# Moving a recurrence's result transposes one step later in an interleaved two-layer Flamingo kernel

## The chip, the cores and the metric

One Trainium2 chip, one of its cores. The metric is device time in microseconds of one execution, median over runs; lower is better. The engines are PE (TensorE, matrix products and transposes), DVE (VectorE), ACT (ScalarE), POOL (GpSimd) and SP (SyncE, which here issues the DMA transfers). [...]

## What is computed

The input x is 4 batch elements of 512 tokens with 512 channels, with a context of the same shape. Two layers follow each other, each a mixing step and a feed-forward step, with gates:

```python
x = x + tanh(g_xattn[0]) * wkv(w, u, layernorm(x), ctx)          # recurrence over tokens
x = x + tanh(g_ffn[0])   * ffn(layernorm(x), w1, w2, w3)          # 512 -> 2048 -> 512
x = x + tanh(g_xattn[1]) * attention(layernorm(x), ctx, wq, bq, wkv, bkv, wp, bp)  # 16 heads
x = x + tanh(g_ffn[1])   * ternary(x, gamma, W)                   # 512 -> 512

# wkv, per channel and token t, with k = layernorm(x), v = ctx
no  = max(o, u + k);  A  = exp(o - no);      E  = exp(u + k - no)
y   = (A * p + E * v) / (A * q + E)
no2 = max(w + o, k);  A2 = exp(w + o - no2); E2 = exp(k - no2)
p, q, o = A2 * p + E2 * v, A2 * q + E2, no2

# ffn: activations rounded to int8 in groups of 64, weights sign(w) * mean|w|
h = silu(bitlinear(x, w1)) * bitlinear(x, w2);  out = bitlinear(h, w3)
```

The attention rounds its query and output inputs per token and those weights per output channel to int8; the ternary step does the same for activations and takes weights to -1, 0, 1.

## The kernel before

P is 128. NB = 4 elements, each 4 token tiles of 128 (NT) by 4 channel blocks of 128 (NC); the hidden 2048 are 4 blocks of 512 (NF).

**The layers.** `wkv_layer` (L551) holds one element's recurrence with channels on partitions and tokens along the row, as 4 chunks of 128 channels (`chunk`, L576). One chunk: a scan on DVE for the running maximum (L588), a subtraction on POOL (L597), ReLUs and exponentials on ACT (L601, L603) into a tile `wk_e` with four 512-long rows, two more scans on DVE (L618, L623), a reciprocal in two halves on DVE (L629), and the product y (L634), which overwrites one row of `wk_e`. PE then transposes y into one PSUM bank `wy_ps` (L636 to L638), and DVE multiplies by the gate and adds into the state `xb` (L640). `wk_e` has a single buffer for elements 1 to 3. For elements 1 to 3 the four chunks are chained by `in_steps(chains, 8)`: chunk c + 1 begins 8 steps after chunk c, and where two chunks have work in one step, the later chunk goes first.

`ffn_layer` (L690) runs 16 units per element, one per (token tile t, hidden block f), in four steps each: `up(t, f, 0)` into a bank `ff_hp` by 8 products, with `gate` behind it (tanh on ACT, L731; DVE, L732); `down` of the unit before the last, 8 products into `ff_acc`, and at f = 3 the addition to `xb` (L759); `up(t, f, 1)` with `gated` (DVE L736 and `quantised`: DVE L231 and L662 to L666, ACT L670, POOL L671); and `gate_parts` of the unit before, which transposes its `ff_z` (`tp_ps`) and splits it in two parts (`hr`: ACT L682, DVE L683). The first element is run with `made`, an object that fetches the weights, takes their signs or rounds them, and turns them, while the units run.

`attention_layer` (L815) is prepared per token tile (`prepared`, L840) and then runs 16 units of (head pair, half), each 8 parts: a score product into a bank `s_ps`, its negative maximum on DVE (`at_nm`, L929), the exponential on ACT (`at_P`, L931), 4 transposes into a bank `pt_ps`, a copy out of it (`at_PT`, L951 on ACT), products with the values (`o_ps`), and a last product and scaling (`ot_ps`, `at_o`, L989). `ternary_layer` (L1123) closes an element.

**The order of the work.** All layers are generators, and each `yield` ends a step. `line` (L1165) gives a generator's steps places on a common scale in which an element's FFN takes 16 of 17 slots; `run` (L1149) always takes the step with the smallest place. Thus FFN of element b + 1, attention of b and recurrence of b + 2 run together. A chunk's eight steps stand 0.05 slot behind FFN steps' places, an attention step 0.05 slot ahead:

```python
(b - 1.0 + 5.05 / SLOTS, b - 1.0 + 13.05 / SLOTS, 32),   # recurrence of b: 4 chunks of 8 steps
(b, b + 16 / SLOTS, 64),                                  # FFN of b: 16 units of 4 steps
start = b + 1 + 4.95 / SLOTS                              # attention of b: 72 steps from here
```

PE's order between steps is written out by hand: `matmul` (L167) and `transpose` (L170) pass each instruction through `in_turn`, and `next_turn` makes what follows stand behind what came before. The order on DVE, ACT, POOL and SP is chosen when the program is built, within the data's dependences and the buffers.

**The banks.** PSUM tiles come from rings by tag: `m` (all transposes by `bank`, and `o_ps`), `hp` (`ff_hp` and `s_ps`) and `acc`:

```python
psum["now"] = boot_ps, {"m": 2, "hp": 2, "acc": 4}   # first element
psum["now"] = ps, {"m": 3, "hp": 3, "acc": 2}        # from then on
```

A tile takes the bank of the one that came so many tiles of its tag before it, and so waits for that one's last reader. For elements 2 and 3 the order on PE around a chunk's end is: `tp_ps`, `wy_ps`, two `s_ps`, `ff_hp` of the next unit's first up, `o_ps`, two `pt_ps`, `ff_acc`.

**Two smaller pieces.** `output_scales` (L424) spreads the weights' scales `sp` (one value per partition and column j) over the rows: a DVE copy `w_full` (L429) of column j broadcast to 128 by 128, then its transpose into `pb_ps` (L430), then a gate product (L431). It runs near the end of the first element (unit 14.7), just after `ternary`, which takes wf to -1, 0, 1 on DVE (L235 to L237) for the transposes `wt_ps`. `prepared` does the same for a token tile's scale: POOL writes `at_full` (L848) into a row ring of three buffers (`at_row`, shared with `at_xn`, `at_q` and `at_half`), PE transposes it into `sx_ps`, and ACT copies it out (L853).

Of the kernel before, what the change touches and what calls it, by code (L numbers as in the profile page):

```python
# [10 lines left out]
F32 = mybir.dt.float32  # L11
# [5 lines left out]
ALU = mybir.AluOpType  # L17
# [4 lines left out]
P = 128  # L22
# [8 lines left out]
def kernel(  # L31
# [36 lines left out]
    nc = tc.nc  # L68
# [68 lines left out]
    def bank(name, dtype=F32):  # L137

        return psum_tile(name, "m", dtype)
# [30 lines left out]
    def transpose(*args):  # L170
        return in_turn(nc.tensor.transpose(*args))  # L171
# [119 lines left out]
    class Weights:  # L291
# [132 lines left out]
        def output_scales(self):  # L424

            pb = bank("pb_ps")
            for j in range(NC):
                full = self.pool.tile([P, P], F32, name="w_full", tag="w_full", bufs=2)
                nc.vector.tensor_copy(full, self.sp[:, j : j + 1].to_broadcast([P, P]))  # L429
                transpose(pb[:, j * P : (j + 1) * P], full, ident)  # L430
            nc.vector.tensor_scalar(swp_b, pb, gates[:, 1:2], None, ALU.mult)  # L431
            nc.sync.dma_start(out=bp_b, in_=bcast(bp))
            nc.vector.tensor_scalar(bp_b, bp_b, gates[:, 1:2], None, ALU.mult)
# [117 lines left out]
    def wkv_layer(b, xb):  # L551

        kT = wk.tile([P, NC, T], F32, name=f"wk_k{b}", tag="wk_k")
        if b:
            r = layernorm(xb, pinned=True)
            yield  # L560
        else:
            r = layernorm(xb)
        for t in range(NT):
            if b or t == 0:
                xn = wk.tile([P, D], F32, name="wk_xn", tag="wk_v")
            else:
                xn = ff.tile([P, D], F32, name="wk_xn", tag="ff_a", bufs=3)
            centred(xn, xb, r, t)
            yield
            pt = bank("wk_ps")  # L570
            for c in range(NC):
                transpose(pt[:, c * P : (c + 1) * P], xn[:, c * P : (c + 1) * P], ident)
            nc.scalar.copy(kT[:, :, t * P : (t + 1) * P], blocks(pt))  # L573

        def chunk(c):
            def row(name):  # L576
                if b == 0 and c % 3:
                    return ff.tile([P, T + 1], F32, name=name, tag=(None, "ff_a", "xp")[c % 3], bufs=3)
                return wk.tile([P, T + 1], F32, name=name, tag=name)

            if b > 1:
                v = wk.tile([P, T], F32, name="wk_v", tag="wk_v")
                nc.sync.dma_start(out=v, in_=cD[b][:, c, :])
            k = kT[:, c, :]
            w_c, u_c, w_n, u_n = (a[:, c : c + 1] for a in (wc, uc, wcn, ucn))
            o = row("wk_o")
            nc.gpsimd.memset(o[:, 0:1], NEG_INF)
            nc.vector.tensor_tensor_scan(  # L588
                o[:, 1:], w_c.to_broadcast([P, T]), k, NEG_INF, ALU.add, ALU.max
            )  # L590

            if b == 0 and c < 3:
                e = ring.tile([P, 4, T], F32, name="wk_e", tag="w")
            else:
                e = wk.tile([P, 4, T], F32, name="wk_e", tag="wk_e")
            z = row("wk_p")[:, 0:T]
            nc.gpsimd.tensor_tensor(z, k, o[:, 0:T], ALU.subtract)  # L597
            if b:
                yield True
            for i, (sign, at) in enumerate(((1.0, u_c), (-1.0, w_c), (-1.0, u_n), (1.0, w_n))):  # L600
                nc.scalar.activation(e[:, i, :], z, AF.Relu, bias=at, scale=sign)  # L601
                if b and i % 2:
                    nc.scalar.activation(  # L603
                        e[:, i - 1 : i + 1, :], e[:, i - 1 : i + 1, :], AF.Exp, scale=-1.0
                    )
                    yield True
            if b == 0:
                exps[c] = nc.scalar.activation(e, e, AF.Exp, scale=-1.0)
                yield True

            A, E2, E, A2 = (e[:, i, :] for i in range(4))
            if b < 2:
                v = context.cT[b][:, c, :]
            q = row("wk_q")
            p = row("wk_p")
            nc.gpsimd.memset(q[:, 0:1], 0.0)
            nc.gpsimd.memset(p[:, 0:1], 0.0)  # L617
            nc.vector.tensor_tensor_scan(q[:, 1:], A2, E2, 0.0, ALU.mult, ALU.add)  # L618
            nc.gpsimd.tensor_tensor(E2, E2, v, ALU.mult)
            den = q[:, 0:T]  # L620
            nc.vector.tensor_tensor(den, A, den, ALU.mult)
            yield True
            nc.vector.tensor_tensor_scan(p[:, 1:], A2, E2, 0.0, ALU.mult, ALU.add)  # L623
            nc.gpsimd.tensor_tensor(den, den, E, ALU.add)
            nc.gpsimd.tensor_tensor(E, E, v, ALU.mult)
            yield True
            for h in range(2):
                half = den[:, h * (T // 2) : (h + 1) * (T // 2)]
                nc.vector.reciprocal(half, half)  # L629
            nc.gpsimd.tensor_tensor(A, A, p[:, 0:T], ALU.mult)  # L630
            nc.gpsimd.tensor_tensor(A, A, E, ALU.add)
            yield True
            y = E2
            nc.vector.tensor_tensor(y, A, den, ALU.mult)  # L634
            yield True
            pt = bank("wy_ps")  # L636
            for t in range(NT):
                transpose(pt[:, t * P : (t + 1) * P], y[:, t * P : (t + 1) * P], ident)  # L638
            xc = xb[:, :, c * P : (c + 1) * P]
            nc.vector.scalar_tensor_tensor(xc, blocks(pt), gates[:, 0:1], xc, ALU.mult, ALU.add)  # L640
            yield True

        chains = [chunk(c) for c in range(NC)]
        if b:
            yield from in_steps(chains, 8)
            return

        for chain in chains:
            next(chain)
            yield  # L650
        yield from in_steps(chains, (0, 1, 2, 4))
# [36 lines left out]
    def ffn_layer(xb, made=None):  # L688
# [16 lines left out]
        def weights(m, f):  # L705
            if made:
                wT[m, f] = made.wT.pop((m, f))
            else:
                wT[m, f] = ring.tile([P, NC, D], F32R, name="wT", tag="w")
                nc.sync.dma_start(out=wT[m, f].bitcast(F32), in_=wD[m][f])  # L710
# [66 lines left out]
            weights(1, 0)  # L777


        for n in range(len(units) + 2):  # L780
            now = n < len(units)
            if now:
                t, f = units[n]
                i = t % size


                if i == min(1, size - 1) and not made:
                    weights(2, f)
                after = units[n + 1] if n + 1 < len(units) else None
                if after and after[1] != f and not made:  # L790
                    weights(0, after[1])
                z = gate(up(t, f, 0))
            yield
            if n > 1:
                down(*units[n - 2])
            yield
            if size == NT and n + 1 < NT:
                inputs_parts(n + 1)
                next_turn()
            if now:  # L800
                gated(t, f, z, up(t, f, 1))
            if now and after and after[1] != f and not made:
                weights(1, after[1])
            yield
            if 0 < n <= len(units):
                gate_parts(*units[n - 1])

            if now and size < NT:
                next_turn()
                if (t, f) in ((0, 1), (1, 2)):  # L810
                    inputs(f + 1)
                elif (t, f) in ((1, 1), (1, 3)):
                    inputs_parts(2 if f == 1 else 3)
            if n < len(units) + 1:
                yield  # L815
# [4 lines left out]
    def attention_layer(b, xb, pool, tiles=range(NT)):  # L820
# [18 lines left out]
        def prepared(t, r):  # L839
            xn = row("at_xn")  # L840
            centred_aside(xn, xb, r, t)
            s = sm.tile([P, 2], F32, name="at_s", tag="at_s")
            yield True
            absmax(s[:, 0:1], xn)
            int8_scale(s[:, 0:1], s[:, 1:2], s[:, 0:1])
            rounded(xn, s[:, 1:2])
            full = row("at_full")[:, 0:P]
            nc.gpsimd.tensor_scalar(full, ones, s[:, 0:1], None, ALU.mult)  # L848
            yield True
            transposed_rows(xqT[:, :, t * P : (t + 1) * P], xn)  # L850
            sp = bank("sx_ps")[:, 0:P]
            transpose(sp, full, ident)
            nc.scalar.copy(sxb[:, t * P : (t + 1) * P], sp)  # L853

            nc.gpsimd.tensor_tensor(xb[:, t, :], xb[:, t, :], bp_b, ALU.add)
            yield True
# [503 lines left out]
```

## Time and profile before

| | us |
|---|---|
| runs, median | 1144.66 |
| runs, lowest and highest | 1143.23 and 1154.57 |
| the profiled execution's own time | 1140.58 |
| its span, first to last instruction | 1138.8 |
| mean granted TensorE clock in it | 0.948 |
| first element with its weights, about | 0 to 352 |
| FFN 1, attention 0, recurrence 2, about | 352 to 620 |
| FFN 2, attention 1, recurrence 3, about | 620 to 800 |
| the rest: FFN 3, attentions 2 and 3, ternary layers | 800 to 1139 |

The stages overlap at their edges. The busy shares of the page are for the whole span. In its views a line "engine line op out<-in xcount | busy, mean ns of one | idle before, releaser" is a group of equal instructions; in a timeline the columns are start, duration, engine, line and operation, tiles, count, and in square brackets how long the engine was idle before it and what it was waiting for by the record. "L171" is the helper through which all transposes go, "L168" the one for all products, so their groups are told apart by the tiles. PEclk is the granted clock of TensorE, 1.00 being full.

### The profile page before, as it was taken

Reading aid. Unit: us, or ns where it says so; the run is one execution under the profiler, and the core shown is the slowest. Engines: PE = TensorE matmul, PEld = TensorE weight load, DVE = VectorE, ACT = ScalarE, POOL = GpSimd, SP = SyncE. Lnnn points to the kernel's source line nnn. Section 1 sums busy time; section 2 is a strip of 40 time slices with the busy share of each in tenths; the row PEclk is TensorE's granted clock in tenths of the full one; section 3 lists DMA queues with packets and bytes.
Section 4 is the critical chain, followed back from the end, with each engine's and each line's share of the span. In section 5 each row is a group of like instructions: output and inputs, shape, how many; then the busy total and the mean of one; then the engine's idle time right before and its main releaser. Section 6 shows DMA issues by size and latency. Waiting matters only on the chain.

```text
span 1138.8 us, 16572 instructions
## 1 busy us (share of the span) xinstructions
PE 967.2 (85%) x5520; PEld 679.9 (60%) x5548; DVE 877.1 (77%) x1889; ACT 722.0 (63%) x1482; POOL 320.4 (28%) x317
## 2 busy tenths in 40 slices
PE   4887898888877968889998897999999899888983
PEld 3344565555555756666776565777777677555651
DVE  5965547679878788999769899977689756688766
ACT  5777555454214576757777677687676577877763
POOL 3821014341305244441124535412122410112000
PEclk8898999999889989999998999999999999998997
DMA  8197745364425545654645544565474572333400
GB/s 277 47 299 281 282 163 184 116 236 148 148 76 192 209 166 177 186 164 169 226 173 185 169 162 137 174 217 163 176 234 149 181 232 76 105 109 103 126 5 37
DMA packets 85668, 189.58 MB, mean 166 GB/s; under 512 B 12240, under 2 KB 36816, under 8 KB 74576
## 3 DMA queue, kind: packets, MB, share of 16 engines
q1 hardware_dynamic: 85584, 188.53, 49.4%
q8 instruction: 44, 0.72, 0.3%
q14 instruction: 40, 0.33, 0.1%
HBM read 148.65 MB, written 39.85 MB: 166 GB/s over the span
## 4 chain that ended last, share of the span: by engine, by line
PE 47%; DVE 27%; ACT 15%; issue 4%; POOL 4%; DMA 2%; SPq 0%; ACTq 0%; POOLq 0%; DVEq 0%
PE ff_hp L168 13%; PE ff_acc L168 7%; PE pt_ps L171 6%; PE o_ps L168 4%; PE s_ps L168 3%; PE v_ps L168 3%; ACT at_P L931 3%; DVE at_nm L929 3%; DVE wk_q L629 3%; DVE qg_i L666 2%; PE qr_ps L171 2%; ACT wk_e L601 2%; PE tp_ps L171 2%; DVE wk_q L618 2%; ACT at_PT L951 2%
## 5 line engine op out<-in xcount | busy, mean ns | idle before, releaser
L168 PE MATMUL ff_hp<-wT,xp 128*128 128x512 f32 x1024 | 275.8, 413 | 5.9 <-ACT at_P L931 2.1
L168 PEld LDWEIGHTS ff_hp<-wT,xp 128*128 128x128 f32 x1024 | 197.0, 196 | 56.4 <-ACT at_P L931 4.6
L931 ACT ACTIVATE at_P<-s_ps,at_nm 128x512 f32<-128x512 f32 x256 | 174.6, 689 | 72.3 <-DVE at_nm L929 71.0
L929 DVE TENSOR_REDUCE at_nm<-s_ps 128x1 f32<-128x512 f32 x256 | 165.8, 678 | 28.5 <-PE s_ps L168 28.3
L671 POOL TENSOR_TENSOR ff_z<-qg_b,qg_s 128x512 f32<-128x512 bf16 x64 | 72.5, 1132 | 335.3 <-ACT qg_b L670 293.0
L951 ACT COPY at_PT<-pt_ps 128x512 f32<-128x512 f32 x224 | 124.0, 596 | 38.5 <-PE pt_ps L171 38.0
L171 PE MATMUL pt_ps<-ident,at_P 128*128 128x128 f32 x1024 | 140.9, 279 | 8.0 <-ACT at_PT L951 2.6
L168 PE MATMUL ff_acc<-wT,hr 128*128 128x512 f32 x512 | 137.9, 411 | 6.1 <-ACT hr L682 3.4
L171 PEld LDWEIGHTS pt_ps<-ident,at_P 128*128 128x128 f32 x1024 | 113.8, 141 | 48.9 <-issue 14.1
L168 PEld LDWEIGHTS ff_acc<-wT,hr 128*128 128x128 f32 x512 | 93.5, 192 | 27.0 <-ACT hr L682 4.3
L168 PE MATMUL s_ps<-at_kR,at_qR 128*128 128x512 f32 x256 | 97.6, 452 | 13.2 <-ACT at_P L931 5.4
L670 ACT CAST qg_b<-qg_i 128x512 bf16<-128x512 int8 x80 | 49.3, 617 | 59.8 <-DVE qg_i L666 53.8
L168 PE MATMUL o_ps<-at_PT,at_V 128*32 128x256 f32 x1024 | 73.0, 399 | 1.8 <-ACT at_PT L951 1.2
L731 ACT ACTIVATE ff_z<-ff_hp,coef 128x512 f32<-128x512 f32 x64 | 43.8, 684 | 46.4 <-PE ff_hp L168 42.9
L736 DVE SCALAR_TENSOR_TENSOR ff_z<-ff_hp,coef,ff_z 128x512 f32<-128x512 f32 x64 | 47.5, 743 | 29.4 <-PE ff_hp L168 29.1
L732 DVE SCALAR_TENSOR_TENSOR ff_z<-ff_z,ff_hp 128x512 f32<-128x512 f32 x64 | 43.6, 681 | 32.7 <-ACT ff_z L731 32.3
L168 PE MATMUL v_ps<-wkvT,cT 128*128 128x512 f32 x128 | 63.2, 642 | 4.2 <-ACT wT L316 3.2
L168 PE MATMUL k_ps<-cT,wkvT 128*128 128x512 f32 x128 | 61.1, 626 | 2.3 <-ACT wk_k L573 1.0
L168 PEld LDWEIGHTS s_ps<-at_kR,at_qR 128*128 128x128 f32 x256 | 45.5, 196 | 28.3 <-ACT at_P L931 13.1
L682 ACT CAST hr<-tp_ps 128x512 fp32r<-128x512 f32 x64 | 37.6, 587 | 35.6 <-PE tp_ps L171 35.6
L629 DVE RECIPROCAL wk_q<-wk_q 128x256 f32<-128x256 f32 x32 | 54.3, 1719 | 1.4 <-POOL wk_p L617 1.4
L171 PE MATMUL tp_ps<-ident,ff_z 128*128 128x128 f32 x256 | 39.9, 279 | 18.1 <-ACT at_PT L951 7.7
(179 smaller groups left out, 1757.3 us busy)
## 6 DMA issues: line engine op xcount, KB each, us to landing
wT<-wD SPq DMA_DIRECT2D x72, 1024.0 KB, 5.2
wn<-in_L_ffn_w_dram SPq DMA_DIRECT2D x18, 1024.0 KB, 6.2
at_kR<-kD SPq DMA_DIRECT2D x128, 128.0 KB, 2.9
at_qR<-qD SPq DMA_DIRECT2D x256, 64.0 KB, 2.2
wD<-wT SPq DMA_DIRECT2D x12, 1024.0 KB, 4.5
kD<-k_half SPq DMA_DIRECT2D x16, 512.0 KB, 3.2
qD<-at_half SPq DMA_DIRECT2D x32, 256.0 KB, 2.0
cn<-in_ctx_dram SPq DMA_DIRECT2D x8, 512.0 KB, 6.2
```

Source lines behind the costliest of these rows:

```text
L168: return in_turn(nc.tensor.matmul(*args, **kwargs))
L171: return in_turn(nc.tensor.transpose(*args))
L629: nc.vector.reciprocal(half, half)
L670: nc.scalar.copy(qb, qi)
L671: nc.gpsimd.tensor_tensor(grouped(src), grouped(qb), s.unsqueeze(2).to_broadcast([P, NG, GS]), ALU.mult)
L682: nc.scalar.copy(part[:, 0, :], pt)
L731: nc.scalar.activation(z, hp, AF.Tanh, scale=coef[:, 0:1])
L732: nc.vector.scalar_tensor_tensor(z, z, 1.0, hp, ALU.add, ALU.mult)
L736: nc.vector.scalar_tensor_tensor(z, hp, coef[:, 1:2], z, ALU.mult, ALU.mult)
L929: nc.vector.tensor_reduce(nm, sp, AX.X, ALU.max, negate=True)
L931: nc.scalar.activation(lanes[k, i, t], sp, AF.Exp, bias=nm, accum_out=sums[k][:, t, i : i + 1],)
L951: made[k] = nc.scalar.copy(dst, blocks(pt))
```

## The change

Four edits, which touch no arithmetic:

1. In `chunk`, for elements 1 to 3, one more `yield True` ahead of the result transposes. A chunk now has 9 steps at a distance of 8, so its transposes fall into the next chunk's first step, after what that step issues. On PE they then stand after the next unit's first up products instead of right after `tp_ps`: `tp_ps`, two `s_ps`, `ff_hp`, `wy_ps`, `o_ps`, two `pt_ps`. A recurrence's last transposes come at the end of its line.
2. In `ffn_layer`, for the first element alone, `down` of the unit before the last stands after the second up products and no longer between the two; a unit keeps four steps.
3. In `output_scales`, the four `w_full` copies are gone; the transposes read the broadcast column of `sp` directly.
4. In `prepared`, the 16 `at_full` operations and their place in the row ring are gone; the transpose reads the broadcast scale directly.

```diff
@@ output_scales
             for j in range(NC):
-                full = self.pool.tile([P, P], F32, name="w_full", tag="w_full", bufs=2)
-                nc.vector.tensor_copy(full, self.sp[:, j : j + 1].to_broadcast([P, P]))
-                transpose(pb[:, j * P : (j + 1) * P], full, ident)
+                transpose(
+                    pb[:, j * P : (j + 1) * P],
+                    self.sp[:, j : j + 1].to_broadcast([P, P]),
+                    ident,
+                )
@@ wkv_layer, chunk
             nc.vector.tensor_tensor(y, A, den, ALU.mult)
             yield True
+            if b:
+                yield True
             pt = bank("wy_ps")
@@ ffn_layer
             yield
-            if n > 1:
-                down(*units[n - 2])
-            yield
+            if not made:
+                if n > 1:
+                    down(*units[n - 2])
+                yield
             if size == NT and n + 1 < NT:
...
             if now and after and after[1] != f and not made:
                 weights(1, after[1])
+            if made:
+                yield
+                if n > 1:
+                    down(*units[n - 2])
             yield
@@ prepared
             rounded(xn, s[:, 1:2])
-            full = row("at_full")[:, 0:P]
-            nc.gpsimd.tensor_scalar(full, ones, s[:, 0:1], None, ALU.mult)
             yield True
             transposed_rows(xqT[:, :, t * P : (t + 1) * P], xn)
             sp = bank("sx_ps")[:, 0:P]
-            transpose(sp, full, ident)
+            transpose(sp, s[:, 0:1].to_broadcast([P, P]), ident)
             nc.scalar.copy(sxb[:, t * P : (t + 1) * P], sp)
```

The counts of instructions on PE, ACT and SP are the same in both programs; DVE has 4 fewer and POOL 16 fewer. The order on DVE, ACT, POOL and SP also shifts around the moved steps.

## The prediction

> **What bounds the kernel now.** First the page's head and its chain of work.
>
> ```profile
> PE 967.2 (85%) x5520; PEld 679.9 (60%) x5548; DVE 877.1 (77%) x1889; ACT 722.0 (63%) x1482; POOL 320.4 (28%) x317
> ...
> PE 47%; DVE 27%; ACT 15%; issue 4%; POOL 4%; DMA 2%; SPq 0%; ACTq 0%; POOLq 0%; DVEq 0%
> ```
>
> PE bounds by the average, with DVE in more than a quarter of the chain. So I looked at windows of about one recurrence chunk each, in the stage where FFN 1, attention 0 and the recurrence of element 2 share the core, and at two short ones in it.
>
> ```profile
> core 0: us, PE busy (x) PEld busy (x) DVE busy (x) ACT busy (x) POOL busy (x), PEclk, DMA share, GB/s
> 418.00:446.00 28.00, 24.44 (x145) 18.79 (x145) 23.23 (x37) 18.72 (x39) 10.92 (x11) 0.90 0.51 165
> 446.00:473.00 27.00, 24.17 (x143) 17.75 (x144) 25.02 (x40) 18.72 (x39) 11.29 (x10) 0.94 0.49 169
> 473.00:500.00 27.00, 22.82 (x144) 17.33 (x145) 26.24 (x54) 18.04 (x39) 13.58 (x14) 0.97 0.56 173
> 436.00:447.00 11.00, 7.87 (x48) 6.52 (x47) 11.00 (x16) 6.27 (x16) 6.35 (x8) 1.00 0.25 78
> 447.40:450.80 3.40, 3.40 (x15) 2.05 (x17) 3.40 (x6) 3.40 (x7) 0.67 (x1) 0.50 0.00 0
> ```
>
> Read PE against DVE. Over a chunk DVE idles 4.8, 2.0 and 0.8 us (28.00 - 23.23 and so on): little room. Over 436 to 447, where a chunk ends, DVE is busy without a break and PE loses 3.1 us. The last row has a granted clock of 0.50. Next the groups by line (window 400 to 780), then the waits of PE.
>
> ```profile
> L171 PE MATMUL wy_ps<-ident,wk_e 128*128 128x128 f32 x32 | 5.9, 315 | 15.7 <-ACT hr L682 11.7 <-DVE wk_e L634 4.1
> ```
>
> ```profile
> PE pb_ps L171 <- DVE w_full L429: 4.7, 2, 4.4
> ```
>
> The result transposes (`wy_ps`) cost 15.7 us of idle PE. The named releaser, `hr` on ACT, is only what ended last: the timeline gives the true one, first PE, then DVE.
>
> ```profile
> 442.18 0.63 PE L171 MATMUL tp_ps<-ident,ff_z 128*128 128x128 f32 x4
> 445.93 0.63 PE L171 MATMUL wy_ps<-ident,wk_e 128*128 128x128 f32 x4 [3.13 <-ACT hr L682]
> 446.38 0.70 PE L168 MATMUL s_ps<-at_kR,at_qR 128*128 128x512 f32 x2
> 446.92 3.23 PE L168 MATMUL ff_hp<-wT,xp 128*128 128x512 f32 x8
> ```
>
> ```profile
> 443.31 1.21 DVE L929 TENSOR_REDUCE at_nm<-s_ps 128x1 f32<-128x512 f32 x2
> 444.45 0.74 DVE L736 SCALAR_TENSOR_TENSOR ff_z<-ff_hp,coef,ff_z 128x512 f32<-128x512 f32 x1
> 445.11 0.68 DVE L634 TENSOR_TENSOR wk_e<-wk_e,wk_q 128x512 f32<-128x512 f32 x1
> ```
>
> DVE's y (L634) ends at 445.79 and PE starts 0.14 later. The same holds at the other stalls: 4.08 us before 417.83, 2.63 before 473.16, 3.00 before 499.29, 2.90 before 691.42 (with 3.13: 15.7). Three chunks (628.8, 662.9, 723.7) and the four of element 1 hardly wait.
>
> **Part 1, the transposes one step later.** On PE they now follow the two score products and up0 (`ff_hp`), so the 15.7 us wait goes. What is late next? Scores and up0 take turns in three `hp` banks, freed by the two `at_P` (L931, ACT) and by L736. At 446 these end 445.33 and 445.19, only 0.5 us ahead of y. With a score product in front, up0 can start 0.4 us after the later, at 445.73 and not 446.92. The transposes, 0.63, then stand behind it. Net for the five stalls, (old up0 start) - (later release + 0.4) - 0.63: 2.1, 0.6, 0.5, 1.3, 1.2, so 5.7 us of the 15.7 at the present clock.
>
> A second limit: with three `m` banks in the order tp, wy, o, pt, pt, the second `pt_ps` inherits the bank of wy, which DVE's `xb` addition (L640) empties. Before, L640 stood near the front of DVE's queue (447.28); in the order of DVE's instructions in the changed program it stands behind two `at_nm`, the quantiser's L666 and L732. From y's end: 1.5 us of small work and `hr` L683, two `at_nm` 1.3, L666 0.6, L732 0.65, L640 0.7, so 4.8, and `pt_ps` at y + 5.0. Old starts of that `pt_ps` are 424.77, 451.90, 477.59, 504.92, 698.09; new ones 422.7, 450.8, 478.0, 504.1, 696.3. Gains 2.1, 1.1, -0.4, 0.8, 1.8, and -0.3 at 662.9: **5.1 us**. This, not the stall, is what I take. The lower end is -4 (eight chunks, half a microsecond each through L640), the upper 10.2, from the clock.
>
> The clock: windows of half clock (as the row at 447.4) follow the gaps of 4.08, 3.13, 3.00 and 2.90 us, none that of 2.63. up0 took 2.46 to 3.62 us in them against 2.09 at full clock, 4.5 us over these up0s. [...] the gaps shrink to some 2 us, and the clock should stay whole. It adds nothing to 5.1 as long as L640 ends last; if not, it gives 5.7 + 4.5 = 10.2.
>
> Also behind the later transposes: the next chunk's ReLUs and exps (L601, L603 on ACT) overwrite y's tile. The first, at 446.64, moves some 3 us. ACT's order puts `at_P` and tanh ahead of them; their reader, the scan L618, came only at 457.5, so I cost this at 0. Without that slack it is up to 3 us a chunk. No DMA is in this step.
>
> **Part 3, w_full removed.** Four DVE copies of 0.22 go, off PE's path but for this:
>
> ```profile
> 320.43 0.38 PE L171 MATMUL pb_ps<-ident,w_full 128*128 128x128 f32 x2
> 325.25 0.47 PE L171 MATMUL pb_ps<-ident,w_full 128*128 128x128 f32 x1 [4.44 <-DVE w_full L429]
> ```
>
> Between, DVE ternarises weights (L235 to L237, 320.04 to 324.40). The third copy waits behind that. Without it PE goes on until `wt_ps`, which reads the same ternary tile `wi`. Before: from tot_ps (ends 318.64) to wt_ps (327.67) 9.0 us. After: up1(14) is already ahead, down(12) 2.1 stands after tot_ps, and its L759 (0.7) lands ahead of the ternary work: 2.1 + 0.7 + some 4.7, so wi at +7.5, wt_ps at +7.65. Gain **1.4**; bounds 0 (wait fully moved) and 7.2 (whole 4.7, and up0 behind it at 2.09 and not 3.62, with 1.0 of the clock on the next). Reading a broadcast as a weight load: the nearest row is the plain load, 0.14 to 0.18; no trace shows a repeated element. Upper bound twice that, 20 loads x 0.16 = 3 us, mostly beside running products. I take no difference.
>
> **Part 2, first element's down behind its second up.** Within a unit nothing is added. At the drain the last up1 (337.25) stood behind an 8-product down (335.10, 2.10 us). Now it is ahead, and the chain L736, quantiser, POOL, `tp_ps` (345.45), down, L759 (351.88), first product of FFN 1 (352.02) starts 2.1 earlier; the down fills the wait. Gain **2.1**, bounds -2 (with two `m` banks and reordered DVE and ACT work a wait of that size can return) and 2.2. The 257 us of this stage from 93 to 350 have 45 us of scattered idle PE; I take the rest as neutral.
>
> **Part 4, at_full removed.** Sixteen POOL operations, 9.7 us, and their claim on the three-buffer row ring. POOL is 28% busy; only element 3's stretch (978) showed sx_ps waiting, 0.24. Gain **0.3**, bounds 0 and 2.
>
> **Sum.** 5.1 + 1.4 + 2.1 + 0.3 = 8.9. Profiled execution 1140.58 (span 1138.8 and 1.8 around it) becomes 1131.7. The median of the runs is 4.1 above that execution: 1144.66 - 8.9 = **1135.8**.
>
> **Rivals.**
> - *The whole wait goes.* L640 is early enough, up0 sets the pace and the clock stays whole: 10.2 + 7.2 + 2.2 + 1 = 20.6, about 1124. For it: every gap near 3 us was followed by half clock. Against: DVE's unbroken 11 us.
> - *The wait only moves.* DVE carries the same work but for four copies, and is full where the stalls are; the wait shows at s_ps, pt_ps and wt_ps. 0 to 3 us left: about 1143.
> - *Slower: L640 takes the wait's place in all eight chunks.* L732, ahead of it, waits for the tanh of the up0 just issued: up0's end + tanh 0.7 + L732 0.7 + L640 0.7 + 0.15 = 2.2; `pt_ps` used to start 1.6 to 1.8 after up0. That is 0.5 a chunk; with ACT's tanh behind an `at_P` (0.68) 1.2, so 8 x 1.2 = 9.6, less 3.8 of the other parts: +5.8, about 1150. It decides once L640 costs over 0.5 us a chunk (8 x 0.5 = 4). Against: at five chunks up0 itself should come earlier.
>
> **How the numbers follow.** Forecast (1130 to 1140) 0.48; whole wait 0.20; only moved 0.20; slower 0.12. The range 1124 to 1149 leaves out some 0.1 at each end: half of the first rival and most of the third above 1149. A measurement here can tell about 1%, 11.4 us: faster means under 1133.2, slower over 1156.1. Faster: nearly all of the first rival and 0.12 of the forecast, 0.31. Slower: the far end of the third, 0.06. The rest, 0.63, within. The forecast's own range is 1130 to 1140.
>
> **What would show it.** Right: no wait before `wy_ps`, up0 0.4 us after the later of `at_P` and L736, a short new wait at `pt_ps` on `xb` L640, no half-clock window at chunk ends, no wait of `pb_ps` but one of `wt_ps` on `wi`, FFN 1's first product about 3.5 us earlier. Wrong: `pt_ps` waiting over 1 us a chunk, scan L618 waiting for the exps, or DVE idle growing in the first element.

## The result, and the profile after

| | before | after |
|---|---|---|
| median of the runs, us | 1143.24 (6 runs) | 1129.62 (6 runs) |
| lowest and highest, us | 1142.21, 1154.57 | 1128.46, 1130.79 |
| ratio after to before, 95% interval | | 0.9865 (0.9827 to 0.9902) |
| profiled execution, its span, us | 1140.58, 1138.8 | 1129.12, 1127.3 |
| mean granted clock | 0.948 | 0.954 |

By the medians the kernel became 13.6 us faster. The ratio is one of means, into which one execution of before with 1154.57 enters; it gives 15.4 (11.2 to 19.8). The two profiled executions differ by 11.5: that of before stood 2.7 us below the median of its runs, that of after only 0.5. A second run of the changed kernel on another chip (below) gave 0.990 (0.9875 to 0.9926). First the page's chain of work after, by engine.

```profile
PE 43%; DVE 29%; ACT 13%; issue 5%; POOL 4%; DMA 4%; SPq 1%; ACTq 0%; POOLq 0%; DVEq 0%
```

PE's share fell from 47% to 43%, DVE's rose from 27% to 29%. The engines' busy times are the same within half a per cent (DVE 877.7 us, ACT 721.4, PE 962.9); only POOL lost its `at_full`. What went is idle time of PE (171.6 to 164.4 us) and some of its busy time (967.2 to 962.9), at a clock of 0.954 and not 0.948; the split is rough, since 28 of PE's records are missing in the trace of before. The waits of PE after show where the old ones went: `wy_ps` keeps one wait, of 1.5 us in the first element, and none at a chunk end. New or larger are these (us in total, times, longest).

```profile
PE s_ps L168 <- ACT at_P L940: 12.7, 15, 2.2
...
PE pt_ps L171 <- ACT at_os L980: 5.1, 6, 2.1
PE wt_ps L171 <- DVE swp_b L433: 5.1, 1, 5.1
```

Before, the first read:

```profile
PE s_ps L168 <- ACT at_P L931: 5.4, 11, 1.2
```

The chunk end that the prediction showed at 442 to 447 is now at 434 to 443, first on PE:

```profile
434.35 0.63 PE L171 MATMUL tp_ps<-ident,ff_z 128*128 128x128 f32 x4
436.89 0.94 PE L168 MATMUL s_ps<-at_kR,at_qR 128*128 128x512 f32 x2 [1.92 <-ACT at_P L940]
437.67 1.98 PE L168 MATMUL ff_hp<-wT,xp 128*128 128x512 f32 x8
439.49 0.60 PE L171 MATMUL wy_ps<-ident,wk_e 128*128 128x128 f32 x4
```

and on DVE:

```profile
435.41 1.21 DVE L938 TENSOR_REDUCE at_nm<-s_ps 128x1 f32<-128x512 f32 x2
436.54 0.73 DVE L741 SCALAR_TENSOR_TENSOR ff_z<-ff_hp,coef,ff_z 128x512 f32<-128x512 f32 x1
437.20 0.67 DVE L636 TENSOR_TENSOR wk_e<-wk_e,wk_q 128x512 f32<-128x512 f32 x1
...
441.72 0.74 DVE L644 SCALAR_TENSOR_TENSOR xb<-wy_ps,gates,xb 128x512 f32<-128x512 f32 x1
```

PE's gap shrank from 3.13 to 1.92 us, and what ends it is the first `at_P`, whose maximum `at_nm` DVE could only take at 435.41. The transposes wait for nothing. Further on the second `pt_ps` waits 0.20 for `at_os`, the copy out of the o_ps bank, on ACT:

```profile
441.88 0.66 PE L171 MATMUL pt_ps<-ident,at_P 128*128 128x128 f32 x4 [0.20 <-ACT at_os L980]
```

```profile
441.44 0.38 ACT L980 COPY at_os<-o_ps 128x256 f32<-128x256 f32 x1
```

Where the time came from, by the start of the same product in both traces (after minus before, profiled executions; the same kernel's two profiles differ by up to 2 us along the way):

| at the start of | before | after | difference |
|---|---|---|---|
| first up of the first element | 100.11 | 101.37 | +1.3 |
| `tot_ps` (sum for the ternary step) | 318.36 | 312.78 | -5.6 |
| `wt_ps` of the ternary tile | 327.67 | 320.96 | -6.7 |
| FFN 1, first transpose | 352.02 | 344.80 | -7.2 |
| FFN 2, first product | 546.44 | 535.81 | -10.6 |
| FFN 3, first product | 769.23 | 757.56 | -11.7 |
| end of the span | 1138.8 | 1127.3 | -11.5 |

### The profile page after: what moved, and what is told of

Same layout as the page of the kernel before. It is cut to its first block, busy times and chain, and to the rows that moved or that the text cites. A ratio compares the mean times of both kernels' runs of the same rounds, so it can differ in the third digit from the quotient of the medians.

```text
span 1127.3 us, 16575 instructions
## 1 busy us (share of the span) xinstructions
PE 962.9 (85%) x5548; PEld 678.1 (60%) x5548; DVE 877.7 (78%) x1885; ACT 721.4 (64%) x1482; POOL 308.8 (27%) x301
## 4 chain that ended last, share of the span: by engine, by line
PE 43%; DVE 29%; ACT 13%; issue 5%; POOL 4%; DMA 4%; SPq 1%; ACTq 0%; POOLq 0%; DVEq 0%
PE ff_hp L168 13%; PE ff_acc L168 6%; PE pt_ps L171 5%; PE o_ps L168 4%; DVE at_nm L938 3%; PE v_ps L168 3%; DVE wk_q L631 3%; PE s_ps L168 3%; ACT at_P L940 3%; DVE qg_i L671 2%; PE tp_ps L171 2%; ACT at_PT L960 2%; PE qr_ps L171 2%; ACT wk_e L603 1%; DMA wn<-in_L_ffn_w_dram 1%
## 5 line engine op out<-in xcount | busy, mean ns | idle before, releaser
L168 PE MATMUL ff_hp<-wT,xp 128*128 128x512 f32 x1024 | 272.3, 410 | 3.1 <-ACT at_P L940 2.1
L168 PE MATMUL s_ps<-at_kR,at_qR 128*128 128x512 f32 x256 | 97.2, 448 | 19.9 <-ACT at_P L940 12.7
```

The costliest lines, as they stand in the source:

```text
L168: return in_turn(nc.tensor.matmul(*args, **kwargs))
```

## The experiments

Each ratio is to the kernel before on the same chip; microseconds are (1 - ratio) times the median of before there (1144.3 to 1146.6).

**One edit at a time, on the kernel before.** The first alone:

```diff
             yield True
+            if b:
+                yield True
             pt = bank("wy_ps")
```

> The kernel before with the first edit alone (result transposes one step later, elements 1 to 3). Theory A, the edits act apart and this one acts at the chunk ends of elements 2 and 3: 5 to 7 us less than before, first element unchanged within 1.5 us. Theory B, the first element's gain of about 7 us comes from element 1's chunks, whose transposes leave PE's queue there: 11 to 13 us less, 5 or more of it before FFN 1 begins. If the wait only moves (the rival of the prediction): under 2 us.

Measured: 0.9932 (0.9906 to 0.9958), 7.8 us less (4.8 to 10.8). Its chunk ends look like those of the full change: three waits of 1.9 to 2.2 us of s_ps on `at_P`, none of wy_ps. FFN 1's first product came 1.3 us later than before, relative to the first up of the first element, so theory B, with the gain in the first element, has nothing for it here.

The second alone:

```diff
-            if n > 1:
-                down(*units[n - 2])
-            yield
+            if not made:
+                if n > 1:
+                    down(*units[n - 2])
+                yield
...
+            if made:
+                yield
+                if n > 1:
+                    down(*units[n - 2])
```

> The kernel before with the second edit alone (first element's down products behind its second up ones). Theory A: 5 to 8 us less, won in the middle of the first element, where down no longer stands between the two ups, and nothing or less in the drain. Theory B: about 2 us, in the drain, as the prediction had it. Nothing should change after FFN 1 has begun but the offset.

Measured: 0.9956 (0.9936 to 0.9976), 5.0 us less (2.7 to 7.3). Its trace puts the gain in the first units, as theory A has it: from the first up to unit 6 7.3 us, then nothing more until FFN 1. Between FFN 1 and FFN 2 this execution lost 4.7 us of it again, at a clock of 0.93 and not 0.96.

The third alone:

```diff
-                full = self.pool.tile([P, P], F32, name="w_full", tag="w_full", bufs=2)
-                nc.vector.tensor_copy(full, self.sp[:, j : j + 1].to_broadcast([P, P]))
+                full = self.sp[:, j : j + 1].to_broadcast([P, P])
```

> The kernel before with the third edit alone (transposes of the scales read the broadcast column). Theory A, the wait for the ternary work moves to the transposes of the ternary tile: 0 to 1.5 us less. Rival, the wait goes with the copies: 4 to 7 us less.

Measured: 0.9976 (0.9960 to 0.9992), 2.7 us less (0.9 to 4.6). In its trace FFN 1's first product comes 1.3 us earlier than before, relative to the first up. The interval meets both theories; its lower half is theory A's.

The fourth alone:

```diff
-            full = row("at_full")[:, 0:P]
-            nc.gpsimd.tensor_scalar(full, ones, s[:, 0:1], None, ALU.mult)
...
-            transpose(sp, full, ident)
+            transpose(sp, s[:, 0:1].to_broadcast([P, P]), ident)
```

> The kernel before with the fourth edit alone (no at_full on POOL, the transpose reads the broadcast scale). Theory A: POOL has room, so 0 to 0.5 us less. Rival, the row ring or POOL holds the start of an attention: 2 us or more less.

Measured: 0.9971 (0.9956 to 0.9985), 3.3 us less (1.7 to 5.0), more than theory A. Its trace shows no place for it: it stays within 2 us of that of before, in parallel, from the first up to the end.

**The changed kernel once more (the control of what follows), and the same without the fourth edit.**

> The changed kernel as it is, for comparison with the three that go with it. 12 to 17 us less than before.

Measured: 0.9900 (0.9875 to 0.9926), 11.4 us less; just below what was expected.

```diff
+            full = row("at_full")[:, 0:P]
+            nc.gpsimd.tensor_scalar(full, ones, s[:, 0:1], None, ALU.mult)
...
-            transpose(sp, s[:, 0:1].to_broadcast([P, P]), ident)
+            transpose(sp, full, ident)
```

> The changed kernel without its fourth edit (at_full on POOL stays). If the fourth edit brings nothing, as its trace says: within 1.5 us of the changed kernel. If the 3 us measured for it alone are real: about 3 us slower than the changed kernel, that is 9 to 12 us less than before.

Measured: 0.9881 (0.9857 to 0.9906), 13.6 us less: no slower than with the edit. Taking it out of the full change cost nothing.

The four edits alone add up to 18.8 us, more than the full change brings. A part of that is clock, which differs between executions of one kernel (0.933 to 0.948 in the 52 of before on that chip). In the executions with a mean granted clock of 0.946 to 0.948 the spans are:

| kernel | executions | mean span, us | less than before |
|---|---|---|---|
| before (three chips) | 15 | 1140.5 | |
| first edit alone | 3 | 1135.9 | 4.6 |
| second alone | 4 | 1137.3 | 3.2 |
| third alone | 3 | 1137.8 | 2.7 |
| fourth alone | 11 | 1140.8 | -0.3 |
| all four (control) | 3 | 1132.0 | 8.4 |
| all but the fourth | 3 | 1131.7 | 8.8 |

At a like clock the edits nearly add, and nothing is left of the fourth: its 22 executions had a mean clock of 0.944, those of before on that chip 0.942. The groups are small, and the clock goes in part with the kernel (on one chip 0.948 to 0.961 in the six executions of the split reciprocal below, 0.935 to 0.947 in the twelve of before), so what an edit gains through it is left out here.

**Does the recurrence of element 1 take part?**

```diff
-            if b:
+            if b > 1:
                 yield True
             pt = bank("wy_ps")
```

> The changed kernel, with the later transposes kept to elements 2 and 3 (element 1 as before). If element 1's chunks take no part in the gain: within 1.5 us of the changed kernel. If they do: 3 us or more slower than it, lost before FFN 1 begins.

Measured: 0.9903 (0.9881 to 0.9925), 11.1 us less, the control's value. There is no sign of it, to within the intervals (some 2.5 us each way); the first edit acts in elements 2 and 3.

**The transposes two steps later**, behind the unit's down products:

```diff
             if b:
                 yield True
+                yield True
             pt = bank("wy_ps")
```

> The changed kernel with the transposes two steps later instead of one, so that they stand behind the unit's down products and no longer between tp_ps and the two pt_ps in the ring of m banks. Bank theory (the later transposes shift the ring, so that the second pt_ps waits for the copy at_os out of the o_ps bank, some 4.5 us over five chunks in the profile after): 2 to 4.5 us less than the changed kernel, and no wait of pt_ps on at_os at the chunk ends. DVE theory (that wait only hides what DVE owes): within 1.5 us. If the ReLUs of the next chunk, which overwrite y's tile, become late: slower, with the scan L618 waiting for ACT.

Measured: 0.9888 (0.9861 to 0.9915), 12.8 us less, 1.4 below the control with overlapping intervals. In six of the eight chunks the transposes now stand behind `ff_acc`, and there `pt_ps` no longer waits for `at_os`; in one of the two with the old order the wait of 0.20 is back. So the wait on `at_os` does come from where the transposes stand; but taking it away is worth little, and s_ps still waits 12.3 us for `at_P` in that trace.

**Is it DVE's work that bounds the chunk ends?** First the second half of the reciprocal is left out in elements 2 and 3 (that half of the result stays undivided):

```diff
-            for h in range(2):
+            for h in range(1 if b > 1 else 2):
                 half = den[:, h * (T // 2) : (h + 1) * (T // 2)]
                 nc.vector.reciprocal(half, half)
```

> The changed kernel without the second half of the reciprocal (1.72 us on DVE) in the eight chunks of elements 2 and 3; that half of the recurrence's result is left undivided. DVE theory (at the chunk ends s_ps waits for banks that at_nm, behind the reciprocal on DVE, lets go late): the 2 us waits of s_ps shrink by about 1.7 each in five chunks, 6 to 11 us less than the changed kernel. PE theory (PE's own work sets the pace, the waits only fill room): within 2 us of it.

Measured: 0.9943 (0.9923 to 0.9963), 6.5 us less than before, so 5 us slower than the control, with 8 x 1.72 = 13.8 us less DVE work. Its trace shows what came in the reciprocal's place. The product y needs POOL's sum L633, and in four of the eight chunks DVE now stood idle for it, 5.8 us in all; in five y took 1.74 to 1.77 us, beside POOL's L599, and not 0.68 as in the others. The first of them:

```profile
412.31 1.77 DVE L636 TENSOR_TENSOR wk_e<-wk_e,wk_q 128x512 f32<-128x512 f32 x1 [1.28 <-POOL wk_e L633]
```

Then a multiplication by 1.0 stands in for both halves, so that nothing is divided there:

```diff
-                nc.vector.reciprocal(half, half)
+                nc.vector.tensor_scalar(half, half, 1.0, None, ALU.mult) if b > 1 else nc.vector.reciprocal(half, half)
```

> The changed kernel, with both halves of the reciprocal in the eight chunks of elements 2 and 3 replaced by a multiplication by 1.0 (their result is left undivided): some 2.6 us less DVE work in a chunk. DVE work theory: 8 to 15 us less than the changed kernel. Queue theory (what decides is what stands ahead of at_nm and of the copies at_PT in the queues of DVE and ACT, which the smaller operation reorders as it did when one half was left out): under 4 us either way, and the s_ps waits at the chunk ends replaced by waits of tp_ps on at_PT.

Measured: 0.9914 (0.9882 to 0.9947), 9.9 us less: no gain over the control, as the queue theory had it. The s_ps waits turned into waits of tp_ps on `at_PT`, 19.5 us in eleven places, the longest 5.12, before 467.94. In ACT's order `at_PT`, which empties the bank that tp_ps takes, stands behind two `at_P` (465.88 and 466.56), of which the first waited 6.00 us for DVE's `at_nm`; so it came at 467.22. What DVE did there, once its two multiplications (460.24, 0.46 us) were done:

```profile
460.63 1.25 DVE L216 TENSOR_SCALAR ln_v<-mv 128x2 f32<-128x2 f32 x1
461.91 0.17 DVE L185 TENSOR_SCALAR rs_half<-ln_v 128x2 int32<-128x2 int32 x1
462.12 1.11 DVE L187 TENSOR_SCALAR rs_y<-rs_half 128x2 int32<-128x2 int32 x1
463.26 1.18 DVE L192 SCALAR_TENSOR_TENSOR rs_t<-rs_y,ln_v 128x2 f32<-128x2 f32 x1
```

and POOL:

```profile
460.40 1.45 POOL L632 TENSOR_TENSOR wk_e<-wk_e,wk_p 128x512 f32<-128x512 f32 x1 [1.51 <-DVE wk_p L625]
461.93 1.27 POOL L633 TENSOR_TENSOR wk_e<-wk_e 128x512 f32<-128x512 f32 x1
463.17 1.26 POOL L599 TENSOR_TENSOR wk_p<-wk_k,wk_o 128x512 f32<-128x512 f32 x1
```

Three layernorm operations on two values a row, elsewhere mostly 0.13 to 0.17 us, took 1.25, 1.11 and 1.18, and each ended within 0.03 us of a POOL operation's end. In the changed kernel's profile the reciprocals (two in 3.33 us from 457.85) and `at_nm` (two in 1.21 from 461.10) ran beside POOL's three; without the reciprocals the small ones did. Of the 4.5 us from the multiplications to `at_nm` (465.16) this is 3.1; the rest is order, for y now stands ahead of `at_nm`. In the two next longest waits (4.30 and 3.58) it is POOL's sum again, with y ahead of `at_nm`:

```profile
682.95 1.73 DVE L636 TENSOR_TENSOR wk_e<-wk_e,wk_q 128x512 f32<-128x512 f32 x1 [1.73 <-POOL wk_e L633]
684.61 1.27 DVE L938 TENSOR_REDUCE at_nm<-s_ps 128x1 f32<-128x512 f32 x2
```

```profile
681.65 1.27 POOL L633 TENSOR_TENSOR wk_e<-wk_e 128x512 f32<-128x512 f32 x1
682.88 1.26 POOL L599 TENSOR_TENSOR wk_p<-wk_k,wk_o 128x512 f32<-128x512 f32 x1
```

So the reciprocal had hidden a wait for POOL, which is the next limit. A plain count of DVE work fails, too: 16 halves at 1.72 - 0.23 are 24 us, and DVE's busy time fell from 877.7 to 869.1.

**The same work in another order.** The second half of the reciprocal one step later, for elements 2 and 3:

```diff
-            for h in range(2):
-                half = den[:, h * (T // 2) : (h + 1) * (T // 2)]
-                nc.vector.reciprocal(half, half)
+            halves = [den[:, h * (T // 2) : (h + 1) * (T // 2)] for h in range(2)]
+            nc.vector.reciprocal(halves[0], halves[0])
+            if b < 2:
+                nc.vector.reciprocal(halves[1], halves[1])
...
             yield True
+            if b > 1:
+                nc.vector.reciprocal(halves[1], halves[1])
             y = E2
```

> The changed kernel with the second half of the reciprocal one step later, for elements 2 and 3: in DVE's order the two at_nm and the gated product now stand between the halves; no work is added or removed. Queue theory: the waits of s_ps at the chunk ends (about 2 us in three to five chunks) shrink by up to 1.7 each, 3 to 8 us less than the changed kernel. DVE work theory: the same total, so within 1.5 us.

Measured: 0.9813 (0.9781 to 0.9844), 21.4 us less than before and 10 less than the control, more than the queue theory had; a value below both intervals of the changed kernel (its own interval lies wholly below that of the control, 0.9875 to 0.9926, and overlaps the first). The same chunk end in its trace, DVE then PE:

```profile
430.64 1.74 DVE L630 RECIPROCAL wk_q<-wk_q 128x256 f32<-128x256 f32 x1
432.31 0.64 DVE L767 SCALAR_TENSOR_TENSOR xb<-ff_acc,coef,xb 128x512 f32<-128x512 f32 x1
432.87 1.27 DVE L941 TENSOR_REDUCE at_nm<-s_ps 128x1 f32<-128x512 f32 x2
434.07 1.73 DVE L637 RECIPROCAL wk_q<-wk_q 128x256 f32<-128x256 f32 x1
```

```profile
435.64 0.63 PE L171 MATMUL tp_ps<-ident,ff_z 128*128 128x128 f32 x4 [0.60 <-ACT at_PT L963]
436.03 0.71 PE L168 MATMUL s_ps<-at_kR,at_qR 128*128 128x512 f32 x2
436.58 1.99 PE L168 MATMUL ff_hp<-wT,xp 128*128 128x512 f32 x8
```

`at_nm` stands between the halves, and s_ps waits for nothing; of the gain 1.48 us go back at 442.08, to `pt_ps` on `at_os`, for ACT's order moved too, and a ReLU (L603, 439.19) now stands ahead of that copy. No work was added or taken away. Over its whole trace s_ps waits 5.6 us for `at_P` and not 12.7, but tp_ps 10.0 for `at_PT` and not 5.8, and pt_ps 6.3 for `at_os` and not 5.1. In sum PE is idle as long as in the changed kernel's profile (164.9 and 164.4 us); what is less is its busy time, 955.5 and not 962.9, at a granted clock of 0.960 and not 0.954. So this profile shows the gain as clock. At a clock of 0.951 one execution of it took 1124.8 us of span, and six of the changed kernel at 0.951 or 0.952 took 1126.4 to 1129.2: some 3 us are left at a like clock. How the new order comes by the better clock was not tried apart.

Both steps together:

```diff
+            if b > 1:
+                nc.vector.reciprocal(halves[1], halves[1])
             y = E2
...
             if b:
                 yield True
+                yield True
             pt = bank("wy_ps")
```

> Transposes two steps later and the second half of the reciprocal one step later, both on the changed kernel. If the two reliefs add: 4 to 10 us less than the changed kernel, and no wait of pt_ps on at_os. If PE's own work bounds by then: no more than the better of the two alone.

Measured: 0.9864 (0.9834 to 0.9894), 15.6 us less: they don't add; the pair is no better than the changed kernel, though its trace has no wait of `pt_ps` on `at_os` at a chunk end. Why is open: its profiled execution was 6.6 us faster than its median, so its trace says little of the loss. The version with the split alone has the lowest time of this study.

## Why the prediction held, and which of its terms did not

The forecast was 1135.8, 8.9 us less; 1129.62 was measured, inside the prediction's range of 1124 to 1149 and just below the forecast's own, 1130 to 1140. The sign and the place of most terms held, but that the total came out so near is in part luck: the forecast terms gave 6.1 of their 8.9 in the traces, and a stage taken as neutral gave more than all of them. In the profiled executions, term by term:

| term | forecast | measured in the trace |
|---|---|---|
| chunk ends, first edit | 5.1 | 4.5 (3.4 to FFN 2, 1.1 to FFN 3) |
| `wt_ps` after `tot_ps`, third edit | 1.4 | 1.1 |
| drain of the first element, second edit | 2.1 | 0.5 |
| middle of the first element | 0 | 6.8 |
| fourth edit | 0.3 | no place found |

**The middle of the first element was the failed step** ("I take the rest as neutral"). From the first up to `tot_ps` it took 218.3 us before and 211.4 after; 5.9 of that is idle time of PE (31.3 to 25.4), at the same clock of 0.95. It repeats: in the four traces without the second edit the stage took 218.3 to 219.1 us, in the ten with it 210.3 to 213.6. The prediction looked at what down waits for and not at what else the moved `yield` carries: with down behind, the next tile's transposes and the second up are issued a quarter of a unit earlier against the other layers' work. Before, on PE, the first up of the second unit, whose tile had been transposed (`tp_ps`) at 108.56:

```profile
112.86 0.50 PE L168 MATMUL ff_hp<-wT,xp 128*128 128x512 f32 x1 [1.60 <-ACT xp L682]
114.35 1.91 PE L168 MATMUL ff_hp<-wT,xp 128*128 128x512 f32 x7 [0.99 <-DVE xp L683]
```

After, where that tp_ps stands at 105.26:

```profile
107.55 3.59 PE L168 MATMUL v_ps<-wkvT,cT 128*128 128x512 f32 x8
110.98 0.39 PE L171 MATMUL wt_ps<-identb,sg 128*128 128x128 bf16 x4
111.17 2.09 PE L168 MATMUL ff_hp<-wT,xp 128*128 128x512 f32 x8
```

Eight value products (`v_ps`) stood ahead of these transposes (104.20) and now stand behind them, so they cover the splitting of `xp` on ACT and DVE. The wait of 1.60 is gone, and the up takes 2.09 us and not 3.40 (112.86 to 116.26, its gap included): 1.6 + 1.3 = 2.9 us, in a unit in which no down is issued at all. The kernel with the second edit alone shows the same order without the wait. The remaining 4 us of this stage are spread, and no single one was tied down.

**The drain** gave 0.5. The last up did come ahead, and from the `wt_ps` after the last `v_ps` (334.91 before, 329.30 after) to FFN 1 the drain is 1.6 us shorter; but that `v_ps` took 4.60 and not 3.60. With the second edit alone the whole drain is 1.8 shorter (24.35 to 22.55). The bound of -2 to 2.2 held.

**The ternary wait moved, as forecast.** On PE after:

```profile
314.84 0.60 PE L171 MATMUL pb_ps<-ident,sp 128*128 128x128 f32 x4
315.28 0.60 PE L171 MATMUL tp_ps<-ident,ff_z 128*128 128x128 f32 x4
320.96 0.58 PE L171 MATMUL wt_ps<-identb,wi 128*128 128x128 bf16 x4 [5.09 <-DVE swp_b L433]
```

From the end of `tot_ps` (313.06) to wt_ps 7.90 us, against 7.65 forecast. The ternary tile was ready at 320.25; the last 0.7 is `swp_b`, behind it on DVE, which empties the bank of pb_ps. Four transposes of a broadcast column take 0.60, no more than four of a full tile at the same clock elsewhere (tp_ps, 0.60), and their loads 0.134 to 0.137 us each: the broadcast cost nothing here.

**The chunk ends: right sum, wrong second limit.** "The second pt_ps inherits the bank of wy" was the step that failed. In the trace L644 ends at 442.46, 4.6 us after y (437.87), close to the 4.8 worked out; but `pt_ps` started at 441.88, before that, and right after `at_os`. So it cannot have taken the bank of wy; its wait says that it took that of o_ps. It waited there in five of the eight chunks, 4.5 us in all (1.14, 0.20, 0.20, 0.87, and 2.13 where ACT had two ReLUs, a cast and an `at_P` ahead of the copy). The slower rival, L640 in the wait's place, did not come; `at_os` on ACT took that place instead, at 4.5 / 8 = 0.6 us a chunk. The forecast of "some 2 us" left of the gaps held for the first three (2.19, 1.92, 2.07); at 490 s_ps waits for nothing, at 679 for 1.2 us, and a wait of 1.69 is new at 617.02. That such a gap depends on the order of the work and not on its amount is what the split reciprocal shows.

And the 4.5 us were not won as the prediction has it, as idle time at the present clock. From FFN 1's first product to FFN 3's, before and after:

```profile
core 0: us, PE busy (x) PEld busy (x) DVE busy (x) ACT busy (x) POOL busy (x), PEclk, DMA share, GB/s
353.37:769.23 415.86, 366.02 (x2185) 275.81 (x2196) 356.39 (x746) 287.05 (x596) 154.25 (x150) 0.96 0.55 182
346.15:757.56 411.41, 361.13 (x2196) 273.72 (x2196) 359.71 (x745) 287.03 (x596) 150.63 (x142) 0.98 0.55 183
```

PE's idle time there is 49.8 us before (at most, for 11 of PE's records are missing) and 50.3 after: what left `wy_ps` came back in other waits, and the stretch is shorter by PE's busy time, that is by clock (0.98 and not 0.96). Other traces scatter: without the first edit the stretch took 414.8 to 420.3 us, of which 49.5 to 52.5 idle (four traces), and with it 411.4 to 416.3, of which 47.7 to 50.3 idle (five traces: after, the first edit alone, the control, and those of the element 1 test and without the fourth edit). In the mean that is 3.5 us, of which 2.5 are idle time: the size of the forecast's 5.1 is roughly right, but a part of it comes as clock, to which the forecast gave nothing.

**The clock did give something.** The prediction let the clock "stay whole" after gaps of 2 us and gave it no value. The five up0s took 3.62, 3.23, 2.02, 2.46 and 3.56 us before, and 2.02, 1.98, 3.57, 1.98 and 2.11 after: 3.2 us less, with one that got slower; so half clock at a chunk end (the 3.57, from 463.36, with 0.50 granted up to 466.80), which the prediction did not expect, did remain. Which one it is changes between executions: in the control's profile the same chunk ends read 2.79, 2.00, 3.21, 3.01 and 2.12.

## What to carry to other kernels

A wait on the critical engine is worth only what the next limit lets through: look up which buffer's release or which queue comes next, and check which bank a tile really takes before pricing a wait on it. A moved step carries everything issued in it, and in an interleaved kernel the work that slides into its place can matter more than what it was moved for. When an engine looks full, try moving its long operations behind the short ones that others wait for before taking work away: the same work in another order brought some 6 to 10 us beyond the change, a part of them as clock, and 24 us less work brought nothing, because POOL's operations were the next limit. And compare executions at a like clock before giving an edit a few microseconds: the fourth measured 3.3 alone, of which a like clock left nothing.

## What the runs showed of the hardware

Some DVE operations took longer beside POOL's. Three layernorm operations with medians of 0.16 to 0.17 us in the profile after (L216, L187, L192) took 1.25, 1.11 and 1.18 where each ended with an operation of POOL, in the trace without division shown above; and y took 1.74 to 1.77 us in five chunks with half a reciprocal, 0.68 in the others. Not all did: L185 (461.91) took 0.17 though POOL's L633 had begun at 461.93, and the reciprocals took 1.69 to 1.75 us in all 32 cases after, the one at 459.49, with POOL's L633 and L599 beside it, 1.69. What decides which of them stretch was not tried apart.

In two places of these traces work that was ready stood behind work that was not, by its engine's order. Before, the banks for `ff_hp` were free at 445.33, but on PE its products stood behind `wy_ps`, which waited 3.13 us and began at 445.93, and two `s_ps`; they began at 446.92. In the trace without division the transposes for `at_PT` were done by 462.44, and on ACT the copy stood behind the two `at_P`, until 467.22.

Half clock came after gaps much shorter than the 2.9 us of the prediction's list: after the changed kernel's gap of 2.07 before 462.59, the windows read (PE, PEld, DVE, ACT, POOL busy, clock, DMA):

```profile
core 0: us, PE busy (x) PEld busy (x) DVE busy (x) ACT busy (x) POOL busy (x), PEclk, DMA share, GB/s
...
460.00:463.40 3.40, 1.33 (x7) 0.80 (x7) 3.40 (x5) 1.88 (x6) 1.96 (x3) 1.00 0.88 333
463.40:466.80 3.40, 3.40 (x10) 2.53 (x10) 3.40 (x9) 0.28 (x1) 0.10 (x1) 0.50 0.01 2
```

From 463.40 to 466.80 PE was granted half, 0.50; up to 463.40 it still had 1.00. The gap of 2.19 before 410.44 had no such sequel (the windows 407.40 to 410.44 and 410.80 to 414.20 both read 1.00), while the same gap in the control, 2.18 before 409.39, was followed by 0.67 from 410.20 to 412.90. So in these profiles the length of a gap alone did not decide.
